# A difference moved to GpSimd, softmax sums from a 129th column, and an earlier order of the first pair's gate products

## The chip, the cores and the metric

The kernel runs on one core of one Trainium2 chip. Time is device microseconds of a whole launch, the median of three runs: 5331.07 us (5317.5 to 5331.74).

## The reference

The input is x (64 x 256 x 128: batch, nodes, features) and adj (256 x 256). Four layers follow, each x = x + layer(relu(layernorm(x))).

```python
# layer 0, five times; in_matrix = out_matrix = adj
m = adj @ h ; av = [m, m]
z = sigmoid(av @ w3.T + b3 + h @ u3.T + bu3) ; r = sigmoid(av @ w4.T + b4 + h @ u3.T + bu3)
hv = tanh(av @ w5.T + b5 + (r * h) @ u5.T + bu5)
h = (1 - z) * h + z * hv
# layer 1: relu of a projection of h, adj-hop and adj-2-hop;  layer 2: adj and a projection, divided by the row's norm
# layer 3: graph attention
e[b,i,j] = sum_e a[e] * leaky_relu(s1[b,i,e] + s2[b,j,e] + b_lin[e]) + adj[i,j]
out = sigmoid(softmax_j(e) @ h)
```

Layer 3 is the large part: for each batch element it needs 256 x 256 x 256 values of a leaky relu, each reduced with the vector a.

## The kernel before, in words

Two batch elements make a pair; there are 32 pairs. Each pair has a front (layers 0 to 2 and the preparation of layer 3, function `front`), 128 tiles of layer 3, and two tails (softmax and product for 128 of the 256 rows i, function `tail`).

**Tiles.** A tile holds, for 4 rows i, 128 of the 256 values of e (half 0 or half 1), 2 batch elements and 256 columns j: 128 partitions x 4 x 512 floats. The leaky relu is written as a linear part (`lin`, made once per pair) and a relu or a minimum. DVE (VectorE) makes a tile with one instruction (L703), ACT (ScalarE) with eight relus of 256 columns (L716), POOL (GpSimd) with eight minima of 256 columns (L723). DVE takes half 0, POOL half 1; ACT takes half 1, and half 0 only where that one is two tiles behind. PE (TensorE) reduces a tile over e with four matmuls in one of two score banks (L760). There are 4096 tiles.

**Front.** One step of layer 0 is: mix with adj (PE, L319), copy mT (ACT, L414), products with u3 and w4 into bank pr (PE), tanh for r into bank r (ACT, L422), rh = (r + 1) * hT (DVE, L426), products with w34, and with w5 and u5 into bank pv (PE, L430 to L434), tanh for z in place (ACT, L437), tanh for hv in place (ACT, L440), d = hv - hT (DVE, L445), pr = (z + 1) * d (DVE, L449), hT = 0.5 * pr + hT (DVE, L453), four transposes (PE, L459) and a copy h (ACT, L464). `norm` (L358) is the layer norm: statistics on DVE, three small operations on POOL, four relus on ACT; it is used four times a front. The banks come from a common store of three (`take`, `spare`); banks 0 and 1 hold s2a, bank 2 a copy of s2n for ACT, banks 3 and 4 the scores.

**Tail.** sc = scores + adj (DVE, L609), + lin (POOL, L613), negative row maximum (DVE, L617), two exponentials with their sums (ACT, L622), transposes (PE), a copy of the weights times 0.5 (ACT, L631), product with h3 (PE), reciprocal of the sums (DVE, L643), tanh with that as scale (ACT, L648), 0.5 * o + 0.5 and + x3 (POOL, L652 and L653), and the output DMA on SP's queue.

**The order.** While the program is written, a planner lays down the order of every engine. Each chain (a front or a tail) is a generator that yields an engine and a time from which its next step may be put; `ran(engine, us, ...)` adds a written-in price (`PROJECT` 0.86, `ELEMENTS` 0.61, `TANH` 0.57, a DVE tile 2.2, 1.05 for L613) to that engine's planned clock. The loop at the end picks the engine with the earliest clock and gives it, in this rank, a step of a tail, a step of a front, or a tile. A front may run ahead only in step with the tiles (`STEPS_OF_FRONT`, `SPREAD`, `AHEAD`); the engines hold at most 8 (DVE), 3 (ACT) and 2 (POOL) finished or begun tiles, of 13 buffers. `in_order` then fixes the order on each engine, so that at run time each goes through its list and waits where an operand isn't there. The fronts of pair 0 and pair 1 start together; no tile can be made before pair 0's is done.

Of the kernel before, what the change touches and what calls it, by code (L numbers as in the profile page):

```python
# [8 lines left out]
F32 = mybir.dt.float32  # L9
AF = mybir.ActivationFunctionType  # L10
OP = mybir.AluOpType
# [3 lines left out]
P = 128  # L15
NB = 2
# [4 lines left out]
PE, DVE, ACT, POOL = ENGINES = (mybir.EngineType.PE, mybir.EngineType.DVE, mybir.EngineType.Activation, mybir.EngineType.Pool)  # L21
# [4 lines left out]
def kernel(  # L26
# [50 lines left out]
    nc = tc.nc  # L77
    B, N, D = x.shape
    NC = N // P
    NPAIR = B // NB  # L80
# [229 lines left out]
    def project(pp, w, t, start=True, stop=True):  # L310

        side_by_side(pp, w, flat(t), start, stop)
# [8 lines left out]
    def to_feature(pt, h):  # L321

        pt = by_token(pt)
        for b in range(NB):
            for c in range(NC):
                nc.tensor.transpose(pt[:, b, c, :], h[:, b, c, :], ident)

    def to_token(pt, ht):

# [28 lines left out]
    def norm(src, since, h):  # L358

        stats = work.tile([P, NB * NC, 6], F32, name="stats")  # L360
        mv = work.tile([P, NB * NC, 2], F32, name="mv")
        s, h = rows_of(src), rows_of(h)
# [28 lines left out]
    def front(p):  # L391
# [5 lines left out]


        h = tok("h", **SHORT)
        t = yield from norm(x0, 9.0 if p else 3.0, h)  # L400
        yield PE, t, 1
        b = take()
        to_feature(b[0], h)
# [4 lines left out]
        for step in range(STEPS):  # L408
            yield PE, t_h, 1, lambda: "adj" in SET_UP
            b = take()  # L410
            mix_nodes(b[0], h, adj_t)
            t = ran(PE, MIX, t_h, b[1])
            yield ACT, t
            mT, t_m = copied("mT", b, t)  # L414
            yield PE, t_m, 1, lambda: "first" in SET_UP
            pr = take()
            project(pr[0], u3t, hT, stop=False)
            project(pr[0], w4t, mT, start=False)
            t = ran(PE, 2 * PROJECT, t_m, t_hT, pr[1])
            yield ACT, t, 1  # L420
            r = take()
# [4 lines left out]
            nc.vector.scalar_tensor_tensor(rh, by_feature(r[0]), 1.0, hT, op0=OP.add, op1=OP.mult)  # L426
            t_rh = ran(DVE, ELEMENTS, t)
            spare.append([r[0], t_rh])
            yield PE, t_rh, 1
            project(pr[0], w34, mT, start=False)  # L430
            t_z = ran(PE, PROJECT, t)
            pv = take()
            project(pv[0], w5t, mT, stop=False)
            project(pv[0], u5t, rh, start=False)  # L434
            t = ran(PE, 2 * PROJECT, t_rh, pv[1])
# [4 lines left out]
            nc.scalar.activation(pv[0], pv[0], AF.Tanh, bias=bh, scale=1.0)  # L440
            t = ran(ACT, TANH, t)

            yield DVE, t
            d = feat("d", **SHORT)
            nc.vector.tensor_sub(d, by_feature(pv[0]), hT)  # L445
            t = ran(DVE, ELEMENTS, t)
            spare.append([pv[0], t])
            yield DVE, max(t_z, clock[DVE])
            nc.vector.scalar_tensor_tensor(by_feature(pr[0]), by_feature(pr[0]), 1.0, d, op0=OP.add, op1=OP.mult)  # L449
            ran(DVE, ELEMENTS, t_z)  # L450
# [5 lines left out]
            spare.append([pr[0], t_hT])  # L456
# [86 lines left out]
        spare.append([po[0], t])  # L543


        h3 = tok("h3")
        t = yield from norm(x3, t, h3)
        yield PE, t, 1
        b = take()
# [55 lines left out]
    def tail(p, ic, pe, since, x3, h3):  # L605

        yield DVE, since
        sc = feat("sc", **SHORT)
        nc.vector.tensor_add(sc, by_feature(pe), adj_n[:, ic, :].unsqueeze(1).to_broadcast([P, NB, N]))  # L609
        t = t_pe[p * NC + ic] = ran(DVE, ELEMENTS, since)  # L610
        ops = READY[p]
        yield POOL, max(t, ops["t_lin"])
        nc.gpsimd.tensor_add(sc, sc, ops["lin"])  # L613
        t = ran(POOL, 1.05, t, ops["t_lin"])
        yield DVE, t
        nmx = work.tile([P, NB], F32, name="nmx")
        nc.vector.tensor_reduce(nmx, sc, AX.X, OP.max, negate=True)  # L617
        t = ran(DVE, ELEMENTS, t)
        yield ACT, t
        sums = work.tile([P, NB], F32, name="sums")  # L620
        for b in range(NB):
            nc.scalar.activation(sc[:, b, :], sc[:, b, :], AF.Exp, bias=nmx[:, b:b + 1], scale=1.0,  # L622
                                 accum_out=sums[:, b:b + 1])
        t_s = ran(ACT, 1.0, t)
        yield PE, t_s, 1
        b = take()
        to_token(b[0], sc)
        t = ran(PE, TURN, t_s, b[1])
        yield ACT, t
        wT = tok("wT", **SHORT)  # L630
        nc.scalar.mul(wT, by_token(b[0]), 0.5)  # L631
        t = ran(ACT, COPY, t)
        spare.append([b[0], t])
        yield PE, t, 1
        b = take()
        po = b[0][:, :NB * D].rearrange("p (b d) -> p b d", b=NB)
# [4 lines left out]
        yield DVE, t_s  # L641
        rs = work.tile([P, NB], F32, name="rs")
        nc.vector.reciprocal(rs, sums)  # L643
        t_s = ran(DVE, 0.08, t_s)
        yield ACT, max(t, t_s)
        o = work.tile([P, NB, D], F32, name="o")
        for k in range(NB):
            nc.scalar.activation(o[:, k, :], po[:, k, :], AF.Tanh, scale=rs[:, k:k + 1])  # L648
        t = ran(ACT, 0.5, t, t_s)
        spare.append([b[0], t])  # L650
        yield POOL, t
        nc.gpsimd.tensor_scalar(o, o, 0.5, 0.5, op0=OP.mult, op1=OP.add)  # L652
        nc.gpsimd.tensor_add(o, o, x3[:, :, ic, :])  # L653
        ran(POOL, 1.1, t)
# [217 lines left out]
```

## Time and profile before

| | |
|---|---|
| median of 3 runs | 5331.07 us |
| the profiled execution | 5330.89 us, span 5329.1 us |
| busy in the span | PE 5227.4, DVE 5209.6, ACT 5132.1, POOL 5153.2 us |
| tiles by engine | DVE 2009, ACT 1423, POOL 664 |
| first tile begun | POOL at 122.72, DVE at 123.51, ACT at 124.00 us |
| last score to the end | 5316.9 to 5329.1 us |

The groups are by line, engine, operation and names of the tiles; "busy" is the time in which at least one instruction of the group ran, the mean is of single instructions. Neighbouring instructions of an engine overlap in the trace, so that the distance of two starts is less than a duration. Idle time is that of the engine just before the group's instructions, with what ended it. A tile of ACT or POOL counts as eight instructions in the trace.

### The profile page before, as it was taken

The numbers are of one execution on the slowest core, as the hardware profiler recorded it, in microseconds if no ns is written. First come the engines' busy times: TensorE is split into PE (matmuls) and PEld (weight loads), VectorE is DVE, ScalarE is ACT, GpSimd is POOL, SyncE is SP. The second block draws the span as 40 slices with busy tenths as digits, with TensorE's granted clock in tenths as the row PEclk, the third lists the DMA queues.
The fourth block names the chain that finished last, engine by engine and source line by source line (L and its number), as shares of the span: only waits on it lengthen the run. The fifth ranks groups of instructions, "written<-read, shape, count | busy, mean of one in ns | idle before, by whom it ended". The sixth has DMA issues, their size and how long they took to land.

```text
span 5329.1 us, 139126 instructions
## 1 busy us (share of the span) xinstructions
PE 5227.4 (98%) x56085; PEld 1861.5 (35%) x56085; DVE 5209.6 (98%) x4313; ACT 5132.1 (96%) x13529; POOL 5153.2 (97%) x5958
## 2 busy tenths in 40 slices
PE   7999999999999999999999999999999999999998
PEld 3333333333333333333333333333333333333332
DVE  4999999999999999999999999999999999999998
ACT  4999999999999999999999999999999999999998
POOL 1999999999999999999999999999999999999999
PEclk9999999999999999999999999999999999999999
DMA  0000000000000000000000000000000000000000
GB/s 19 7 8 5 8 7 6 8 5 8 8 5 8 7 6 8 7 6 8 5 8 7 6 8 6 6 8 7 6 8 5 8 7 6 8 5 6 6 5 4
DMA packets 60344, 37.49 MB, mean 7 GB/s; under 512 B 4528, under 2 KB 59696, under 8 KB 59696
## 3 DMA queue, kind: packets, MB, share of 16 engines
q1 hardware_dynamic: 58976, 28.59, 2.3%
q8 instruction: 438, 7.18, 0.6%
q14 instruction: 210, 1.72, 0.1%
q10 hardware_dynamic: 720, 0.00, 0.0%
HBM read 18.09 MB, written 10.49 MB: 5 GB/s over the span
## 4 chain that ended last, share of the span: by engine, by line
DVE 44%; PE 31%; POOL 15%; issue 5%; ACT 5%; DMA 0%; POOLq 0%; DVEq 0%; SPq 0%; ACTq 0%
DVE rl L703 36%; PE bank L760 20%; POOL rl L723 13%; PE bank L305 10%; ACT rl L716 4%; DVE stats L365 1%; DVE bank L449 1%; DVE d L445 1%; DVE rh L426 1%; DVE hT L453 1%; PE bank L333 1%; POOL mv L300 1%; POOL sc L613 1%; DVE mv L368 1%; DVE nmx L617 0%
## 5 line engine op out<-in xcount | busy, mean ns | idle before, releaser
L723 POOL TENSOR_SCALAR rl<-s2n,s1b 128x256 f32<-128x256 f32 x5312 | 4779.4, 953 | 9.5 <-ACT s1b L590 9.3
L703 DVE TENSOR_TENSOR rl<-s1a,bank 128x2048 f32<-128x2048 f32 x2009 | 4468.7, 2275 | 11.7 <-ACT s1a L599 11.7
L716 ACT ACTIVATE rl<-bank,s1b 128x256 f32<-128x256 f32 x11072 | 4409.4, 903 | 1.0
L760 PE MATMUL bank<-rl,win_n 128*32 128x512 f32 x21384 | 2659.7, 594 | 38.0 <-DVE rl L703 31.2
L760 PE MATMUL bank<-rl,win 128*32 128x512 f32 x11384 | 1511.8, 594 | 0.0
L760 PEld LDWEIGHTS bank<-rl,win_n 128*32 128x32 f32 x21384 | 682.5, 110 | 1512.9 <-issue 1214.9
L760 PEld LDWEIGHTS bank<-rl,win 128*32 128x32 f32 x11384 | 369.1, 110 | 749.5 <-issue 618.6
L305 PE MATMUL bank<-mT,wts 128*32 128x512 f32 x2560 | 335.0, 593 | 1.4 <-DVE d L445 0.6
L305 PE MATMUL bank<-adj_t,h 128*32 128x256 f32 x5120 | 308.5, 381 | 4.6 <-ACT h L464 3.5
L305 PEld LDWEIGHTS bank<-adj_t,h 128*32 128x32 f32 x5120 | 165.2, 110 | 174.8 <-issue 52.2
L376 ACT ACTIVATE h<-x,mv 128x128 f32<-128x128 f32 x384 | 171.3, 626 | 35.5 <-POOL mv L372 35.2
L382 ACT COPY mT<-bank 128x512 f32<-128x512 f32 x160 | 146.4, 915 | 39.0 <-PE bank L305 30.5
L305 PE MATMUL bank<-hT,wts 128*32 128x512 f32 x1280 | 168.3, 593 | 0.0
L305 PE MATMUL bank<-mT,w 128*32 128x512 f32 x1280 | 166.8, 593 | 1.3 <-ACT bank L422 1.3
L305 PE MATMUL bank<-rh,u5t 128*32 128x512 f32 x1280 | 166.6, 592 | 0.0
L422 ACT ACTIVATE bank<-bank,gate_b 128x512 f32<-128x512 f32 x160 | 150.8, 942 | 13.8 <-PE bank L305 13.5
L437 ACT ACTIVATE bank<-bank,gate_b 128x512 f32<-128x512 f32 x160 | 145.9, 912 | 16.2 <-PE bank L305 16.1
L440 ACT ACTIVATE bank<-bank,gate_b 128x512 f32<-128x512 f32 x160 | 147.3, 921 | 12.0 <-PE bank L305 10.6
L464 ACT COPY h<-bank 128x512 f32<-128x512 f32 x128 | 132.2, 1033 | 19.8 <-PE bank L333 19.8
L305 PEld LDWEIGHTS bank<-mT,wts 128*32 128x32 f32 x2560 | 82.0, 110 | 196.3 <-issue 142.4
L716 ACT ACTIVATE rl<-s2c,s1a 128x256 f32<-128x256 f32 x312 | 148.5, 891 | 0.0
L300 POOL TENSOR_TENSOR mv<-mv,minus_half 128x4 f32<-128x4 f32 x128 | 133.0, 1039 | 10.7
(113 smaller groups left out, 3204.7 us busy)
## 6 DMA issues: line engine op xcount, KB each, us to landing
xin<-in_x_dram SPq DMA_DIRECT2D x64, 128.0 KB, 2.2
lin<-row SPq DMA_DIRECT2D x32, 256.0 KB, 7.6
out_dram<-o SPq DMA_DIRECT2D x64, 128.0 KB, 1.8
row<-quarter SPq DMA_DIRECT2D x32, 64.0 KB, 1.5
w_raw<-in_L_gnn_w_w_dram SPq DMA_DIRECT2D x3, 128.0 KB, 2.7
th_raw<-in_L_gnn_Theta_dram SPq DMA_DIRECT2D x1, 320.0 KB, 3.9
adj_n<-in_adj_dram SPq DMA_DIRECT2D x1, 256.0 KB, 3.5
w_raw<-in_L_gnn_u_w_dram SPq DMA_DIRECT2D x2, 64.0 KB, 2.9
```

The costliest lines, as they stand in the source:

```text
L300: nc.gpsimd.tensor_tensor(t, t, minus_half, op=OP.pow)
L305: nc.tensor.matmul(o[g:g + 32], w[:, g:g + 32], t, start=start, stop=stop, skip_group_check=True)
L376: nc.scalar.activation(h[:, k, :], s[:, k, :], AF.Relu, bias=mv[:, k, 0:1], scale=mv[:, k, 1:2])
L382: nc.scalar.copy(c, by_feature(bank[0]))
L422: nc.scalar.activation(r[0], pr[0], AF.Tanh, bias=br, scale=0.5)
L437: nc.scalar.activation(pr[0], pr[0], AF.Tanh, bias=bz, scale=0.5)
L440: nc.scalar.activation(pv[0], pv[0], AF.Tanh, bias=bh, scale=1.0)
L464: nc.scalar.copy(h, by_token(b[0]))
L703: nc.vector.tensor_tensor(t, rows.to_broadcast(whole), ops["s2a"].unsqueeze(1).to_broadcast(whole), op=OP.min)
L716: nc.scalar.activation(t[:, g, b, :], (s2p if k else ops["s2c"])[:, b, :], AF.Relu, bias=ops["s1"][k][:, b, i:i + 1], scale=-1.0)
L723: nc.gpsimd.tensor_scalar(t[:, part, b, :], ops["s2n"][:, b, :], ops["s1"][1][:, b, i:i + 1], None, op0=OP.min)
L760: nc.tensor.matmul(pe[g * 32:(g + 1) * 32, :], w[:, k, 31 - r:63 - r], flat(t[:, g]), start=first, stop=(left[block] == 0), skip_group_che ...
```

## The change

Four things change, and the planner's order with them.

1. In layer 0 of all pairs but the first, tanh for hv is written to SBUF (d), POOL subtracts hT in place, planned at 1.3 us, and the bank pv is given back after the tanh. In the first pair the difference stays on DVE.
2. h3 gets a 129th column that holds 2.0 (a memset on POOL per pair). The exponentials write no sums; the product with h3 is 129 columns wide, and its last column is twice the sum. The reciprocal reads that column from the bank, so it comes after the product. The copy of the weights isn't scaled any more.
3. In the first pair, u3's product is put as soon as hT is there, w4's and w5's as soon as mT is there, w34's after the tanh for r, u5's after rh. Its pr, r and pv are banks 3, 2 and 4, which no tile uses yet, instead of banks from the store. The front of the second and later pairs is planned to begin at 20.0 us instead of 9.0.
4. In the last tail of all, the addition of lin and the last two operations are on DVE. In the other tails the planner's price of POOL's addition of lin is 1.3 instead of 1.05 us.

```diff
-        t = yield from norm(x0, 9.0 if p else 3.0, h)
+        t = yield from norm(x0, 20.0 if p else 3.0, h)
...
+            if p == 0:
+                pr, r, pv = ([banks[k], 0.0] for k in (3, 2, 4))
+                yield PE, t_hT, 0, lambda: "first" in SET_UP
+                project(pr[0], u3t, hT, stop=False)
+                ran(PE, PROJECT, t_hT)
+                yield PE, t_m
+                project(pr[0], w4t, mT, start=False)
+                t = ran(PE, PROJECT, t_m)
+                project(pv[0], w5t, mT, stop=False)
+                ran(PE, PROJECT)
+                yield ACT, t
...
+            if p == 0:
+                yield PE, t
+                project(pr[0], w34, mT, start=False)
+                t_z = ran(PE, PROJECT, t)
+                yield PE, t_rh
+                project(pv[0], u5t, rh, start=False)
+                t = ran(PE, PROJECT, t_rh)
...
-            nc.scalar.activation(pv[0], pv[0], AF.Tanh, bias=bh, scale=1.0)
-            nc.vector.tensor_sub(d, by_feature(pv[0]), hT)
...
+            if p < 1:
+                nc.scalar.activation(pv[0], pv[0], AF.Tanh, bias=bh, scale=1.0)
+                t = ran(ACT, TANH, t)
+                yield DVE, t
+                nc.vector.tensor_sub(d, by_feature(pv[0]), hT)
+                t = ran(DVE, ELEMENTS, t)
+            else:
+                nc.scalar.activation(d, by_feature(pv[0]), AF.Tanh, bias=bh, scale=1.0)
+                t = ran(ACT, TANH, t)
+                spare.append([pv[0], t])
+                yield POOL, t
+                nc.gpsimd.tensor_sub(d, d, hT)
+                t = ran(POOL, 1.3, t)
+            yield DVE, max(t, t_z)
             nc.vector.scalar_tensor_tensor(by_feature(pr[0]), by_feature(pr[0]), 1.0, d, op0=OP.add, op1=OP.mult)
...
-        h3 = tok("h3")
+        h3 = work.tile([P, NB, NC, D + 1], F32, name="h3")
+        nc.gpsimd.memset(h3[:, :, :, D:D + 1], 2.0)
...
+        end = (p, ic) == (NPAIR - 1, NC - 1)
+        if end:
+            yield DVE, max(t, ops["t_lin"])
+            nc.vector.tensor_add(sc, sc, ops["lin"])
+            t = ran(DVE, ELEMENTS, t, ops["t_lin"])
+        else:
+            yield POOL, max(t, ops["t_lin"])
+            nc.gpsimd.tensor_add(sc, sc, ops["lin"])
+            t = ran(POOL, 1.3, t, ops["t_lin"])
...
-            nc.scalar.activation(sc[:, b, :], sc[:, b, :], AF.Exp, bias=nmx[:, b:b + 1], scale=1.0,
-                                 accum_out=sums[:, b:b + 1])
+            nc.scalar.activation(sc[:, b, :], sc[:, b, :], AF.Exp, bias=nmx[:, b:b + 1], scale=1.0)
...
-        nc.scalar.mul(wT, by_token(b[0]), 0.5)
+        nc.scalar.copy(wT, by_token(b[0]))
...
-        po = b[0][:, :NB * D].rearrange("p (b d) -> p b d", b=NB)
+        po = b[0][:, :NB * (D + 1)].rearrange("p (b d) -> p b d", b=NB)
...
-        nc.vector.reciprocal(rs, sums)
+        nc.vector.reciprocal(rs, po[:, :, D])
...
+        yield DVE if end else POOL, t
+        e = nc.vector if end else nc.gpsimd
+        e.tensor_scalar(o, o, 0.5, 0.5, op0=OP.mult, op1=OP.add)
+        e.tensor_add(o, o, x3[:, :, ic, :])
```

More of the change, by code (lines that the diff above doesn't have):

```diff
@@ L325, in to_feature @@
             for c in range(NC):
-                nc.tensor.transpose(pt[:, b, c, :], h[:, b, c, :], ident)
+                nc.tensor.transpose(pt[:, b, c, :], h[:, b, c, 0:D], ident)
     def to_token(pt, ht):
@@ L361, in norm @@
         mv = work.tile([P, NB * NC, 2], F32, name="mv")
-        s, h = rows_of(src), rows_of(h)
+        s, h = rows_of(src), rows_of(h)[:, :, 0:D]
         yield DVE, since
@@ L414, in front @@
             mT, t_m = copied("mT", b, t)
[L415 to L421, printed above, removed]
+            if p == 0:
[10 more added lines that the diff above has]
+            else:
+                yield PE, t_m, 1, lambda: "first" in SET_UP
+                pr = take()
+                project(pr[0], u3t, hT, stop=False)
+                project(pr[0], w4t, mT, start=False)
+                t = ran(PE, 2 * PROJECT, t_m, t_hT, pr[1])
+                yield ACT, t, 1
+                r = take()
             nc.scalar.activation(r[0], pr[0], AF.Tanh, bias=br, scale=0.5)
@@ L427, in front @@
             t_rh = ran(DVE, ELEMENTS, t)
[L428 to L435, printed above, removed]
+            if p == 0:
[6 more added lines that the diff above has]
+            else:
+                spare.append([r[0], t_rh])
+                yield PE, t_rh, 1
+                project(pr[0], w34, mT, start=False)
+                t_z = ran(PE, PROJECT, t)
+                pv = take()
+                project(pv[0], w5t, mT, stop=False)
+                project(pv[0], u5t, rh, start=False)
+                t = ran(PE, 2 * PROJECT, t_rh, pv[1])
             yield ACT, t_z
@@ L439, in front @@
             yield ACT, t
-            nc.scalar.activation(pv[0], pv[0], AF.Tanh, bias=bh, scale=1.0)
-            t = ran(ACT, TANH, t)
-            yield DVE, t
             d = feat("d", **SHORT)
[L445 to L448, printed above, removed]
+            if p < 1:
[4 more added lines that the diff above has]
+                t = ran(DVE, ELEMENTS, t)
+            else:
+                nc.scalar.activation(d, by_feature(pv[0]), AF.Tanh, bias=bh, scale=1.0)
[5 more added lines that the diff above has]
+            yield DVE, max(t, t_z)
             nc.vector.scalar_tensor_tensor(by_feature(pr[0]), by_feature(pr[0]), 1.0, d, op0=OP.add, op1=OP.mult)
-            ran(DVE, ELEMENTS, t_z)
+            ran(DVE, ELEMENTS, t, t_z)
             yield DVE, clock[DVE]
@@ L455, in front @@
             t_hT = ran(DVE, ELEMENTS)
-            spare.append([pr[0], t_hT])
+            if p > 0:
+                spare.append([pr[0], t_hT])
             yield PE, t_hT, 1
@@ L611, in tail @@
         ops = READY[p]
-        yield POOL, max(t, ops["t_lin"])
-        nc.gpsimd.tensor_add(sc, sc, ops["lin"])
-        t = ran(POOL, 1.05, t, ops["t_lin"])
+        end = (p, ic) == (NPAIR - 1, NC - 1)
[3 more added lines that the diff above has]
+            t = ran(DVE, ELEMENTS, t, ops["t_lin"])
+        else:
+            yield POOL, max(t, ops["t_lin"])
+            nc.gpsimd.tensor_add(sc, sc, ops["lin"])
+            t = ran(POOL, 1.3, t, ops["t_lin"])
         yield DVE, t
@@ L619, in tail @@
         yield ACT, t
-        sums = work.tile([P, NB], F32, name="sums")
         for b in range(NB):
-            nc.scalar.activation(sc[:, b, :], sc[:, b, :], AF.Exp, bias=nmx[:, b:b + 1], scale=1.0,
-                                 accum_out=sums[:, b:b + 1])
-        t_s = ran(ACT, 1.0, t)
+            nc.scalar.activation(sc[:, b, :], sc[:, b, :], AF.Exp, bias=nmx[:, b:b + 1], scale=1.0)
+        t_s = ran(ACT, 0.8, t)
         yield PE, t_s, 1
@@ L640, in tail @@
         t = ran(PE, PRODUCT, t, b[1])
-        yield DVE, t_s
+        yield DVE, t
         rs = work.tile([P, NB], F32, name="rs")
-        nc.vector.reciprocal(rs, sums)
-        t_s = ran(DVE, 0.08, t_s)
-        yield ACT, max(t, t_s)
+        nc.vector.reciprocal(rs, po[:, :, D])
+        t = t_s = ran(DVE, 0.15, t)
+        yield ACT, t
         o = work.tile([P, NB, D], F32, name="o")
         for k in range(NB):
-            nc.scalar.activation(o[:, k, :], po[:, k, :], AF.Tanh, scale=rs[:, k:k + 1])
+            nc.scalar.activation(o[:, k, :], po[:, k, 0:D], AF.Tanh, scale=rs[:, k:k + 1])
         t = ran(ACT, 0.5, t, t_s)
         spare.append([b[0], t])
[L651 to L654, printed above, removed]
+        yield DVE if end else POOL, t
+        e = nc.vector if end else nc.gpsimd
+        e.tensor_scalar(o, o, 0.5, 0.5, op0=OP.mult, op1=OP.add)
+        e.tensor_add(o, o, x3[:, :, ic, :])
+        ran(DVE, 0.6, t) if end else ran(POOL, 1.1, t)
         nc.sync.dma_start(out[p * NB:(p + 1) * NB, ic * P:(ic + 1) * P, :].rearrange("b p d -> p b d"), o)
```

## The prediction

> **What bounds the kernel now.** I read the page's busy shares first, then busy time by stretch, then the instruction groups of the long middle stretch, then one timeline of it. Time by stretch (columns: stretch, length, busy us and instructions of each engine, granted TensorE clock, DMA share, GB/s):
>
> ```profile
> 0.00:123.00 123.00, 95.49 (x1057) 39.50 (x1057) 45.09 (x125) 46.24 (x82) 9.61 (x24) 0.93 0.07 19
> 150.00:5000.00 4850.00, 4808.85 (x52044) 1712.92 (x52040) 4827.20 (x3968) 4745.67 (x12528) 4801.07 (x5545) 1.00 0.03 7
> 5317.00:5329.10 12.10, 3.12 (x36) 1.96 (x36) 1.41 (x3) 2.32 (x7) 2.39 (x3) 0.63 0.04 11
> ```
>
> There are 123 us before the first tile, in which VectorE (DVE) works 45; a middle of 4850 us in which DVE is idle 22.8 us (0.5%), TensorE (PE) 41.2, GpSimd (POOL) 48.9 and ScalarE (ACT) 104.3; and 12 us after the last score. The middle is 91% of the time, and no engine in it has 3% to spare. These groups of it (busy us, mean ns; idle us before them and who ended it) say where DVE's little idle time lies:
>
> ```profile
> L703 DVE TENSOR_TENSOR rl<-s1a,bank 128x2048 f32<-128x2048 f32 x1866 | 4152.6, 2275 | 0.0
> L449 DVE SCALAR_TENSOR_TENSOR bank<-bank,d 128x512 f32<-128x512 f32 x149 | 103.2, 693 | 2.3
> L445 DVE TENSOR_TENSOR d<-bank,hT 128x512 f32<-128x512 f32 x149 | 100.9, 677 | 0.4 <-ACT bank L440 0.4
> L617 DVE TENSOR_REDUCE nmx<-sc 128x2 f32<-128x512 f32 x59 | 40.1, 679 | 8.2 <-POOL sc L613 8.1
> L613 POOL TENSOR_TENSOR sc<-sc,lin 128x512 f32<-128x512 f32 x59 | 78.3, 1326 | 0.0
> ```
>
> DVE never waits for a tile buffer (L703: 0.0); 8.2 of its 22.8 us are waits for POOL's addition of `lin`, which the planner prices at 1.05 us. A duration overstates an operation's price, since neighbours overlap; starts give it:
>
> ```profile
> 2503.39 0.68 DVE L609 TENSOR_TENSOR sc<-bank,adj_n 128x512 f32<-128x512 f32 x1
> 2503.99 0.68 DVE L426 SCALAR_TENSOR_TENSOR rh<-bank,hT 128x512 f32<-128x512 f32 x1
> 2504.59 2.27 DVE L703 TENSOR_TENSOR rl<-s1a,bank 128x2048 f32<-128x2048 f32 x1
> ...
> 2507.05 1.30 POOL L613 TENSOR_TENSOR sc<-sc,lin 128x512 f32<-128x512 f32 x1
> 2508.30 12.62 POOL L723 TENSOR_SCALAR rl<-s2n,s1b 128x256 f32<-128x256 f32 x14
> ...
> 2508.99 6.67 DVE L703 TENSOR_TENSOR rl<-s1a,bank 128x2048 f32<-128x2048 f32 x3
> ...
> 2513.35 4.95 ACT L716 ACTIVATE rl<-bank,s1b 128x256 f32<-128x256 f32 x12
> ```
>
> So a 128x512 operation of DVE costs 0.60 (2503.99 - 2503.39), a DVE tile (6.67 - 2.275)/2 = 2.20, POOL's quarter of 256 columns (12.62 - 0.953)/13 = 0.90, POOL's 128x512 addition 1.25, up to its mean 1.33, and ACT's 256 columns (4.95 - 0.9)/11 = 0.37.
>
> **What the skill says.** SBUF — State Buffer, Who interferes with whom: a DVE instruction with at most one SBUF input doesn't contend with GpSimd. The tile (s1a from SBUF, the other operand in a bank) and `d` are such; 2.20 a tile beside an always busy POOL agrees. GPSIMD Engine Reference, Elementwise: a two-input addition takes 1.96 times as long there as on DVE; here 1326 against 679 ns, 1.95. Perfetto Trace Analysis, Identifying the Most-Contended Engine: matmul busy time is a poor measure of headroom; so I don't take PE's 98% as proof that it binds.
>
> **The change, part by part.** The counts are those of the changed program's order.
>
> *Difference on POOL.* 155 of 160 `d` leave DVE: -155 x 0.60 = -93. The planner gives the room to tiles: DVE 2009 to 2046, +37 x 2.20 = +81. POOL: +155 x 1.28 = +198 (mean of 1.25 and 1.33 less overlap), tiles 5312 to 5064 quarters: -248 x 0.90 = -223. ACT: 11384 to 11336 relus, -48 x 0.37 = -18; of them the dearer ones from SBUF fall from 312 to 16 (891 against 903 ns in the groups' means, so taken at nothing). The tanh now writes SBUF instead of a bank; the nearest row, s1a from a bank to SBUF, runs at the same pace, so 0 (+/- 0.02 x 155 = 3, on ACT, which has 104 spare). The bank pv comes free one DVE operation earlier.
>
> *129th column.* 128 accumulator reads leave ACT. Two exponentials with their reads take 2509.32 to 2510.31 = 0.99 in the timeline, two bare activations 2 x 0.4 = 0.8: -64 x 0.19 = -12. PE: 1024 matmuls one column wider, +1/128 of 71 us busy = +0.6. The reciprocal now waits for the product and reads a bank; on DVE 0.08 becomes 0.08 to 0.2, I take 0.15: +64 x 0.07 = +4.5. It lies between product and last tanh; behind it on DVE stand tiles, with buffers in reserve, and the spare bank is held longer by about this. 32 memsets of 4 columns on POOL: 0.1 each (as its constants at the start), +3.
>
> *First pair.* In the start, u3's product already ran in the shadow of the copy of mT (PE 54.20, copy 54.45 to 55.04, w4 at 55.09). Only w5's 0.86 us between w34 and u5 is on the chain: 5 x 0.86 = 4.3 us to gain. But the second pair's instructions are laid between differently. I walked the new order by hand with the durations and handoffs of the old timeline (PE to ACT 1.1 after a product's start, 2.0 after a mix; ACT copy to PE 0.64; tanh to DVE 0.70; DVE to DVE 0.72). The second step: hT 21.1, transposes 22.0, h 22.7, mix 23.4; but pair 1's norm now stands on ACT ahead of mT (25.5 to 27.15), so mT 27.15 instead of 25.4; w4 27.8, r 28.95; PE lays pair 1's mix in (29.5 to 31.2), w34 31.2, u5 32.1, tanh 33.2, d 33.9, update 34.6, hT 35.3. In the fourth step mT is ready for PE at 53.8, but pair 1's w34, w5 and u5 are ahead: w4 at 57.2. The five new hT of pair 0 start at 21.1, 35.3, 48.5, 62.2, 77.6; before 21.09, 34.63, 48.48, 62.05, 77.74. Afterwards 0.9 us is won at the theta products. The matmuls ahead of the first tile are the same in kind and number in both orders. Gain 1 us; bounds +4 and -3.
>
> *Last softmax.* sc starts at 5316.87, nmx at 5318.94; with `lin` on DVE nmx starts after 2 x 0.72 (two dependent DVE operations): -0.6. Exponentials without reads -0.2; the reciprocal in the path +0.4; the last two operations 0.42 + 0.29 on DVE (128x256 and a cheaper one by their set-up rows) instead of 0.41 + 0.72: -0.5; handoffs -0.3. Together -1.2. The last DMA is issued that much earlier; no other DMA moves on SP's queue but with its producer.
>
> *Planner's price of `lin`*, 1.05 to 1.30: POOL's 1.28 fits now. Of the 8.2 us of DVE waits I let 7 go (bounds 4 and 8).
>
> *New wait.* The update L449 (now L476) waits for POOL instead of for DVE's own `d`; behind it are hT, DVE's tiles of 2.2 us, and on PE the transposes of hT. POOL takes `d` up between quarters of 0.90 us, and DVE is planned to come when it is done, so only lateness against plan costs. The nearest row is nmx behind POOL's sc: 8.2/59 = 0.14 us each with a price 0.23 short. With a right price I take 0.03: +155 x 0.03 = +5; bounds 0 and 0.14 x 155 = 21. The old gap between d and update (2.3 us) goes.
>
> **Sum on DVE**, the engine with least room: -93 + 81 + 4.5 = -7.5; waits -7 - 2.3 + 5 = -4.3; start -1; end -1.2: -14. POOL has -22 and ACT -30 of work; ACT's waits of 104 us come partly from POOL lateness (h behind mv 27 us, nmx 13.5), so I add -3 for steadier handoffs that DVE sees through banks. -17. The profiled execution took 5330.89 (span 5329.1, 1.8 outside it); the median is 5331.07, as good as equal. 5331 - 17 = **5314**. Here 0.3% is 16 us, about what a measurement of this kernel can tell: the forecast stands on that line.
>
> **Rivals.**
> B, DVE isn't the bound alone. The three engines' work falls by 7.5 + 22 + 30 = 60, and PE idles 41 us in the middle. If the balance is shared, lateness shrinks everywhere: half of PE's 41 goes besides the 1 + 1.2 and the 7: 5331 - 30 = 5301. For: PE's waits are spread over all three engines. Against: DVE took all of half 0 but 2 tiles, and can't shed them.
> C, new waits take the room: 0.10 us at each of 155 handoffs instead of 0.03, 11 us more, and 3 for banks held longer by the reciprocal: 5328. For: the nearest row's 0.14. Against: its price was short.
> D, slower: POOL falls behind its plan. Its norm costs 0.236 + 1.039 + 0.201 and two idle gaps of 0.08, 1.6 us for the planned 1.4, four times a pair, and DVE now meets POOL five more times a pair. If each costs 0.35 us (some 0.4 of a quarter), 54 instead of 5: 5363. Slower by 0.3% is 5347, 33 above the forecast, so it decides from (33 + 5)/155 = 0.25 us each. Against: DVE waited 4.9 us in all for rn and little for mv.
>
> **Chances.** Forecast 0.45 (its own range 5307 to 5321), B 0.22, C 0.23, D 0.10. Faster by over 0.3% (under 5315): half of the forecast's and B, 0.46; within: the other half and C, 0.44; slower 0.10. Low 5294: B with all but a few of the 41 (5331 - 9 - 41 = 5281 is its end); high 5334: C at 0.14 each (21 instead of 5, and 3). Outside lie D and the rest of B, under 0.2.
>
> **What would show it.** DVE idle in the middle under 20 us; nmx behind sc under 2; the update behind POOL's d under 8; the first DVE tile at 121 to 125; POOL's d at 1.25 to 1.33 us; 12 us after the last score becoming 11. Wrong if the first tile moves by over 5 us, if DVE idles over 40, or if L703's 2.275 changes.

## The result and the profile after

The changed kernel takes **5299.72 us** (median of 4 runs, 5299.0 to 5300.57), the kernel before 5331.13 (4 runs, 5317.5 to 5331.74). The ratio is 0.9943, 95% interval 0.993 to 0.9955: faster, by 31 us where the forecast had 17. The spread of the kernel before is taken up in the last section. The profiled execution has a span of 5298.6 us, 30.5 less than before.

First the changed kernel by stretch (columns as in the prediction: length, busy us and instructions of PE, its weight loads, DVE, ACT and POOL, clock, DMA share, GB/s):

```profile
0.00:123.00 123.00, 96.47 (x1057) 39.34 (x1057) 43.12 (x121) 48.88 (x88) 18.71 (x33) 0.96 0.08 20
150.00:5000.00 4850.00, 4824.62 (x52264) 1720.98 (x52266) 4837.71 (x3868) 4730.55 (x12415) 4800.93 (x5512) 1.00 0.03 7
5287.00:5298.60 11.60, 3.39 (x37) 1.99 (x36) 2.96 (x6) 2.12 (x5) 0.00 (x0) 0.62 0.04 11
```

Length less busy time is idle time. In the middle DVE's falls from 22.8 to 12.3 us and PE's from 41.2 to 25.4, POOL's stays (48.9 and 49.1), ACT's grows from 104.3 to 119.5. For the whole span, DVE's time can be closed as an account: busy 5209.6 to 5194.6, -15.0; idle -15.5, of which the middle gives -10.5, the stretch from 5000 to 5287 us (5317 before) -4.4, the last tail behind it -2.0, and the first 150 us +1.5.

The groups of the middle that answer to those shown of before (busy us, mean ns; idle us just before them and who ended it):

```profile
L737 DVE TENSOR_TENSOR rl<-s1a,bank 128x2048 f32<-128x2048 f32 x1913 | 4250.9, 2276 | 0.0
L476 DVE SCALAR_TENSOR_TENSOR bank<-bank,d 128x512 f32<-128x512 f32 x149 | 103.0, 691 | 2.5 <-POOL d L473 2.3
L652 DVE TENSOR_REDUCE nmx<-sc 128x2 f32<-128x512 f32 x59 | 39.8, 675 | 0.4 <-POOL sc L648 0.4
L568 DVE SCALAR_TENSOR_TENSOR x<-bank,rn,x 128x128 f32<-128x128 f32 x120 | 33.6, 342 | 0.9 <-POOL rn L300 0.6
L676 DVE RECIPROCAL rs<-bank 128x2 f32<-128x2 f32 x59 | 9.7, 164 | 0.1
L473 POOL TENSOR_TENSOR d<-d,hT 128x512 f32<-128x512 f32 x150 | 196.9, 1312 | 0.3 <-ACT d L469 0.3
```

nmx waits 0.4 us for POOL instead of 8.2, the sum x behind rn (the inverse norm of layer 2, made on POOL) 0.9 instead of the 4.9 it had in the kernel before:

```profile
L540 DVE SCALAR_TENSOR_TENSOR x<-bank,rn,x 128x128 f32<-128x128 f32 x120 | 33.5, 339 | 4.9 <-POOL rn L300 4.9
```

The new wait, the update (L476) behind POOL's d, costs 2.5, about what the old gap between d and update (2.3) had cost. A DVE tile is what it was (2276 against 2275 ns) although POOL has 155 more additions with two SBUF inputs: what the Trainium skill says in SBUF — State Buffer, Who interferes with whom, of DVE instructions with at most one SBUF input agrees here too. (The page excepts the 2-port performance modes, in which DVE takes the ports it shares with GpSimd; the prediction leaves that out. Whether the small operation in the last section is such a case, no run shows.)

One handoff of it, from the timeline (start, length, engine and line):

```profile
2495.07 1.04 ACT L469 ACTIVATE d<-bank,gate_b 128x512 f32<-128x512 f32 x1
2495.22 0.67 DVE L652 TENSOR_REDUCE nmx<-sc 128x2 f32<-128x512 f32 x1
2495.82 4.47 DVE L737 TENSOR_TENSOR rl<-s1a,bank 128x2048 f32<-128x2048 f32 x2
2497.45 1.30 POOL L473 TENSOR_TENSOR d<-d,hT 128x512 f32<-128x512 f32 x1
2498.72 7.21 POOL L757 TENSOR_SCALAR rl<-s2n,s1b 128x256 f32<-128x256 f32 x8
2500.21 0.68 DVE L476 SCALAR_TENSOR_TENSOR bank<-bank,d 128x512 f32<-128x512 f32 x1
2500.81 2.27 DVE L737 TENSOR_TENSOR rl<-s1a,bank 128x2048 f32<-128x2048 f32 x1
2503.01 0.15 DVE L676 RECIPROCAL rs<-bank 128x2 f32<-128x2 f32 x1
2503.09 0.66 DVE L480 SCALAR_TENSOR_TENSOR hT<-bank,hT 128x512 f32<-128x512 f32 x1
```

What the prediction calls POOL's quarter is one of the eight minima of 256 columns that make up a tile. The tanh ends at 2496.11; POOL takes d up at 2497.45, after the four minima that its order lays ahead of it (from 2493.87), and has it ready at 2498.75. DVE makes two tiles meanwhile and comes at 2500.21, 1.5 us after that: no wait. The reciprocal, which now reads a bank, costs 0.08 from start to start (2503.09 - 2503.01).

### The profile page after: what moved, and what is told of

Its sections match the earlier page's. It is cut to its first block, busy times and chain, and to the rows that moved or that the text cites. A ratio compares the mean times of both kernels' runs of the same rounds, so it can differ in the third digit from the quotient of the medians.

```text
span 5298.6 us, 138351 instructions
## 1 busy us (share of the span) xinstructions
PE 5215.3 (98%) x56085; PEld 1855.4 (35%) x56085; DVE 5194.6 (98%) x4198; ACT 5093.4 (96%) x13353; POOL 5126.0 (97%) x5894
## 5 line engine op out<-in xcount | busy, mean ns | idle before, releaser
L757 POOL TENSOR_SCALAR rl<-s2n,s1b 128x256 f32<-128x256 f32 x5064 | 4565.0, 943 | 11.4 <-ACT s1b L619 8.9
L737 DVE TENSOR_TENSOR rl<-s1a,bank 128x2048 f32<-128x2048 f32 x2046 | 4545.1, 2276 | 10.6 <-ACT s1a L628 10.6
L750 ACT ACTIVATE rl<-bank,s1b 128x256 f32<-128x256 f32 x11320 | 4538.6, 923 | 2.5 <-PE bank L794 1.3
L794 PE MATMUL bank<-rl,win 128*32 128x512 f32 x11336 | 1493.5, 593 | 0.0
L473 POOL TENSOR_TENSOR d<-d,hT 128x512 f32<-128x512 f32 x155 | 203.3, 1311 | 53.2 <-ACT d L469 53.2
L457 ACT ACTIVATE bank<-bank,gate_b 128x512 f32<-128x512 f32 x160 | 167.0, 1044 | 19.5 <-PE bank L305 19.5
L469 ACT ACTIVATE d<-bank,gate_b 128x512 f32<-128x512 f32 x155 | 166.7, 1076 | 7.3 <-PE bank L305 7.3
L434 ACT ACTIVATE bank<-bank,gate_b 128x512 f32<-128x512 f32 x160 | 152.9, 955 | 13.4 <-PE bank L305 12.8
L300 POOL TENSOR_TENSOR mv<-mv,minus_half 128x4 f32<-128x4 f32 x128 | 133.3, 1041 | 10.7
```

The costliest lines, as they stand in the source:

```text
L300: nc.gpsimd.tensor_tensor(t, t, minus_half, op=OP.pow)
L469: nc.scalar.activation(d, by_feature(pv[0]), AF.Tanh, bias=bh, scale=1.0)
L473: nc.gpsimd.tensor_sub(d, d, hT)
L737: nc.vector.tensor_tensor(t, rows.to_broadcast(whole), ops["s2a"].unsqueeze(1).to_broadcast(whole), op=OP.min)
L750: nc.scalar.activation(t[:, g, b, :], (s2p if k else ops["s2c"])[:, b, :], AF.Relu, bias=ops["s1"][k][:, b, i:i + 1], scale=-1.0)
L757: nc.gpsimd.tensor_scalar(t[:, part, b, :], ops["s2n"][:, b, :], ops["s1"][1][:, b, i:i + 1], None, op0=OP.min)
```

## The experiments

The experiments form three sets, each measured on a chip of its own with the kernel before beside it: the four undone parts; the changed kernel again with three loads; and the price alone, the other two loads and the last version. There the kernel before takes 5318.22, 5318.48 and 5318.71 us, and the changed kernel, measured in the second set alone, 5290.53 (5 runs, 5290.45 to 5291.33; ratio 0.9948, 0.9936 to 0.996). In their profiles POOL's minima are 0.896 to 0.898 us apart, in the first two profiles 0.899; a DVE tile takes 2.20 everywhere. Below, "+" and "-" are against these 5290.53 or 5318.71. Each ratio, to the kernel before of the same set, has an interval of up to 0.0013 to both sides, 7 us; the runs of one kernel lie within 4 us, one run each of the price alone and of the kernel before apart, and differences under 2 us are taken as none. The expectations of the first set still count from the 5300 of the first measurement: only their differences are to be compared.

The theory: the kernel before lost time because POOL was behind its plan and DVE waited for it; DVE's work sets the pace, and POOL is nearly as full. The main rivals: rival B of the prediction (PE shares the bound); that the gain is the first pair's, or the column's; that the price alone is worth nothing.

### One part undone in the changed kernel

**The difference on DVE in all pairs.**

```diff
-            if p < 1:
+            if p < NPAIR:
...
                 t = ran(DVE, ELEMENTS, t)
+                if p > 0:
+                    spare.append([pv[0], t])
```

> The changed kernel (5300 us) with one part undone: the difference stays on DVE in all pairs, all else as changed. Tiles go back to DVE 2010, ACT 11392/8, POOL 5296/8. If DVE with its waits is the bound, it gets back the work it lost (busy 5194.6 to about 5208), so +13 to +18: 5313 to 5318, with DVE idle in the middle staying near 12 us. If the three engines share the bound, their work rises by 15 + 20 + 18 and a third of that is 18: 5318, so the two theories agree here and only the size of this part is read. If the planner's price was the whole gain: 5303 or less.

Measured: 5305.11 us (5303.11 to 5306.11), ratio 0.9974 (0.9964 to 0.9985), +14.6. That is in the range expected, where both theories put it. In the order DVE has 2010 tiles instead of 2046, POOL 5296 minima instead of 5064. With the 0.608 us that a difference and what it adds to the update behind it cost in the first pair of profiles (below), an estimate of DVE's work is 155 x 0.608 - 36 x 2.197 = +15.1. The trace has less: DVE is busy 5200.8 instead of 5189.3 us, +11.5, and idle 3.9 us more (in the middle 11.6 against 8.9). So most of this part is work, and a quarter of it waits.

**The sums by the accumulator, as before.** The memset, the 129th column and the late reciprocal go; the exponentials write sums and the copy is scaled by 0.5.

```diff
-            nc.scalar.activation(sc[:, b, :], sc[:, b, :], AF.Exp, bias=nmx[:, b:b + 1], scale=1.0)
-        t_s = ran(ACT, 0.8, t)
+            nc.scalar.activation(sc[:, b, :], sc[:, b, :], AF.Exp, bias=nmx[:, b:b + 1], scale=1.0,
+                                 accum_out=sums[:, b:b + 1])
+        t_s = ran(ACT, 1.0, t)
...
-        nc.vector.reciprocal(rs, po[:, :, D])
-        t = t_s = ran(DVE, 0.15, t)
+        nc.vector.reciprocal(rs, sums)
+        t_s = ran(DVE, 0.08, t_s)
```

> The changed kernel with the exponentials' accumulated sums back and no 129th column. It gives ACT 12 us of work and takes nothing worth naming from DVE (the reciprocal measured 164 against 161 ns). If DVE is the bound: 5300, no change within 2 us. If the bound is shared: a third of 12, 5304. If banks held longer by the late reciprocal cost anything: below 5298.

Measured: 5295.97 us (5294.52 to 5297.84), ratio 0.9958 (0.9946 to 0.9971), +5.4, nearer to the 4 us expected of a shared bound than to none. But the middle is the same (DVE busy 4842.39 of 4850 us, 4841.14 in the changed kernel). The loss is in one place, the last tiles, of which DVE's start and the first operation of the last tail are, in this kernel:

```profile
5239.48 33.08 DVE L738 TENSOR_TENSOR rl<-s1a,bank 128x2048 f32<-128x2048 f32 x15
5281.98 0.69 DVE L637 TENSOR_TENSOR sc<-bank,adj_n 128x512 f32<-128x512 f32 x1 [9.42 <-PE bank L795]
```

and in the changed kernel measured again:

```profile
5235.16 39.63 DVE L737 TENSOR_TENSOR rl<-s1a,bank 128x2048 f32<-128x2048 f32 x18
5277.77 0.69 DVE L638 TENSOR_TENSOR sc<-bank,adj_n 128x512 f32<-128x512 f32 x1 [2.98 <-PE bank L794]
```

DVE's last tile ends at 5272.56 (5239.48 + 33.08), 2.2 us earlier than at 5274.79, and then DVE waits 9.42 us for the last scores instead of 2.98: the tiles still missing are other engines'. So 6.4 us come from how the planner happened to deal out the last tiles, more than the whole difference. What the column itself is worth isn't shown; by this subtraction it is next to nothing.

**The old first pair.** Product order, banks and 9.0 us as before.

```diff
-        t = yield from norm(x0, 20.0 if p else 3.0, h)
+        t = yield from norm(x0, 9.0 if p else 3.0, h)
...
-            if p == 0:
+            if p < 0:
```

> The changed kernel with the first pair's products in the old order, in banks from the store, and the second pair planned from 9.0 us again. The first DVE tile came 2.6 us earlier with the change; if that is all that this part does: 5302.5, with the first DVE tile at 123.5. If the gain at the start is owed to something else (the clock granted to PE): 5300.

Measured: 5289.46 us (5289.07 to 5289.67), ratio 0.9946 (0.9933 to 0.9958), -1.1, where +2.5 with the first tile at 123.5 was expected. No gain comes from the new order of the first pair. DVE's first tile is at 120.37 with the old order and at 120.50 with the new one; with the difference on DVE (above) it is at 124.91. So the first tile comes earlier through the second pair's differences leaving DVE, not through the products.

**The old price of lin**, 1.05 instead of 1.3.

```diff
-            t = ran(POOL, 1.3, t, ops["t_lin"])
+            t = ran(POOL, 1.05, t, ops["t_lin"])
```

> The changed kernel with the planner's price of POOL's addition of lin back at 1.05 us (it takes 1.31). If the price ended POOL's lateness: nmx waits for sc come back (0.4 to about 8 us on DVE), those of x for rn as well (0.9 to 5): 5310 to 5314. If the gain comes from less work alone: 5300 to 5302.

Measured: 5299.71 us (5298.25 to 5300.84), ratio 0.9965 (0.9952 to 0.9977), +9.2. The waits are back, in the middle, as expected if the price ended POOL's lateness, though not in full: nmx 5.0 us, x behind rn 2.4, the update behind d 2.9; DVE idles 17.6 us there instead of 8.9.

```profile
L652 DVE TENSOR_REDUCE nmx<-sc 128x2 f32<-128x512 f32 x59 | 40.2, 681 | 5.0 <-POOL sc L648 4.9
```

The four undone parts give 14.6 + 5.4 - 1.1 + 9.2 = 28.1; the whole change is worth 5318.5 - 5290.5 = 28.0. That they meet so closely is in part chance, since the 5.4 are the dealing of the last tiles. The end of the last tail was undone in none of them.

### The whole change again, and the price alone

> The changed kernel as it is, for its place beside the runs of the same call. Each of the first four experiments ran on a chip where the kernel before took 5318 instead of 5331, and there POOL's quarter tile started every 0.896 us instead of 0.899 while DVE's tile stood at 2.197: 5064 x 0.003 is 15 us. If POOL sets the pace, the changed kernel moves with the chip like the kernel before, and the ratio stays at 0.994: 5287 on the faster chip, 5300 on the slower one. If DVE sets it: near 5300 on both.

That is the 5290.53 above, with the ratio at 0.9948: it lies nearer to what was expected if POOL sets the pace (5287) than to DVE alone (near 5300). With DVE's tile unchanged, the kernel became 9.2 us faster. In DVE's account of the two profiles 5.3 us of this are busy time (5194.6 to 5189.3) and 4.6 idle time, and 3.9 of the 5.3 lie in one small operation that runs in step with POOL (last section). So POOL's pace, or something that changed with it, reaches the time through DVE. Its middle, against which the experiments are read:

```profile
150.00:5000.00 4850.00, 4829.90 (x52341) 1725.83 (x52344) 4841.14 (x3875) 4731.34 (x12440) 4796.74 (x5521) 1.00 0.03 7
```

**The kernel before with the new price**, nothing else:

```diff
-        t = ran(POOL, 1.05, t, ops["t_lin"])
+        t = ran(POOL, 1.3, t, ops["t_lin"])
```

> The kernel before with one number changed: the planner's price of POOL's addition of lin is 1.30 instead of 1.05 us. The order gives POOL 5296 quarters instead of 5312 and DVE the same 2009 tiles, so hardly any work moves. Theory (POOL late against its plan was a cost of the kernel before in its own right, and the price alone takes it away): nmx's wait for POOL in the middle falls from 8.2 to under 2 us, and the time by about 9 us, what taking the price out of the changed kernel cost. Rival (the price is worth something only together with the difference on POOL; before, DVE has its full work whatever it waits for): the wait goes, and the time stays within 3 us of the kernel before.

Measured: 5307.34 us (5305.83 to 5314.41), ratio 0.9979 (0.9972 to 0.9987), -11.4 against the kernel before. Its profiled execution is the one at 5314.41, with POOL's minima 0.898 us apart, so it is to be read beside the first two profiles. Its middle, by stretch and by groups:

```profile
150.00:5000.00 4850.00, 4816.51 (x52168) 1721.71 (x52164) 4837.72 (x3976) 4761.16 (x12571) 4803.63 (x5551) 1.00 0.03 7
```

```profile
L617 DVE TENSOR_REDUCE nmx<-sc 128x2 f32<-128x512 f32 x59 | 39.9, 676 | 2.5 <-POOL sc L613 2.4
L540 DVE SCALAR_TENSOR_TENSOR x<-bank,rn,x 128x128 f32<-128x128 f32 x120 | 33.5, 338 | 1.1 <-POOL rn L300 1.0
```

DVE idles 12.3 us instead of 22.8, as little as in the changed kernel's first profile. One number in the planner, which moves two tiles from POOL to ACT, takes most of the middle's waits away; the rival that it is worth nothing alone falls. nmx's wait came to 2.5, not under 2.

### An engine loaded

Each of these adds work to one engine once a pair (32 times): an operation on a scratch tile, or on PE the s2a product a second time into the same bank. The planner doesn't know of it. What it adds is its distance from start to start.

```diff
# one of:
+        nc.gpsimd.tensor_tensor(idle_p, idle_p, minus_half, op=OP.pow)
+        nc.vector.tensor_reduce(idle_v[:, 960:961], idle_v[:, 0:960], AX.X, OP.max)
+        nc.scalar.activation(idle_a, idle_a, AF.Relu, scale=1.0)
+        project(s2a, w2n[:, 0:P], hT)
```

> The changed kernel with one more power of 128x4 on POOL per pair (1.04 us, 33 us in all), on a scratch tile that nothing waits for, without a price, so that the order of all the rest stays. If POOL sets the pace: +25 to +33 against the changed kernel of this call. If DVE sets it: POOL has 49 us idle in the middle, of which 29 lie between its own dependent operations, so +0 to +13. If all share: about a third, +11.

> The same with one more maximum over 960 columns on DVE per pair (960 columns at 0.6 us per 512 are about 1.05 us, 34 in all), unpriced. If DVE sets the pace: +28 to +34. If POOL does: DVE has 12 us idle in the middle and 3 after it, so it takes the lead once these are used up: +15 to +20 at most. If all share: +11.

> The same with one more relu of 1024 columns on ACT per pair (about 1.0 us, 32 in all), unpriced. ACT has 119 us idle in the middle, so if POOL or DVE sets the pace: +0 to +6. If all share: +11. If ACT's handoffs set it: over +20.

> The changed kernel with the s2a product of each pair done twice on PE, into the same bank and with the same values: 32 x 0.86 = 27.5 us of PE's time. Theory (DVE sets the pace, PE has room that the tiles in reserve cover): under 0.3 of it, +8 us at most, with PE idle in the middle falling from 25 us to near nothing. Rival B of the prediction (PE shares the bound, and its idle time is what shrinks): 0.7 of it or more, +19 to +28 us, and tiles' buffers held longer, seen as DVE and POOL waiting for PE.

> The kernel before with one more power of 128x4 on POOL in each pair, on a scratch tile, not priced: 32 x 0.996 = 31.9 us of POOL's time, and no other engine's. In the changed kernel the same addition cost 24.5 us, 0.77 of itself. Theory (POOL shared the pace of the kernel before at least as much as it does that of the changed one): +25 to +32 us, and DVE's waits behind POOL (nmx, x behind rn) more than double. Rival (DVE alone set the pace before; POOL's relief was worth nothing): under +12 us.

Measured:

| loaded | added us | time us (range) | ratio (interval) | more by | share |
|---|---|---|---|---|---|
| changed, DVE | 33.9 | 5323.32 (5322.72 to 5325.19) | 1.001 (1.0001 to 1.0018) | 32.8 | 0.97 |
| changed, POOL | 31.9 | 5315.01 (5314.41 to 5317.19) | 0.9994 (0.9986 to 1.0002) | 24.5 | 0.77 |
| changed, PE | 28.1 | 5296.35 (5295.36 to 5297.98) | 0.9959 (0.9946 to 0.9971) | 5.8 | 0.21 |
| changed, ACT | 30.7 | 5295.38 (5295.19 to 5295.99) | 0.9957 (0.9945 to 0.997) | 4.9 | 0.16 |
| before, POOL | 31.9 | 5346.97 (5346.78 to 5348.06) | 1.0054 (1.0041 to 1.0068) | 28.3 | 0.89 |

DVE sets the pace, POOL nearly so, PE and ACT don't. DVE alone, for which 0 to 13 us were expected of the load on POOL, doesn't fit the 24.5. Rival B's reason falls with the 0.21: PE's idle time in the middle shrinks with the load (20.1 to 5.6 us), and the time hardly grows:

```profile
150.00:5000.00 4850.00, 4844.41 (x52544) 1733.14 (x52540) 4836.29 (x3871) 4730.36 (x12426) 4793.05 (x5517) 1.00 0.03 7
```

That POOL's work comes through DVE's waits is seen in the changed kernel with POOL loaded:

```profile
L478 DVE SCALAR_TENSOR_TENSOR bank<-bank,d 128x512 f32<-128x512 f32 x149 | 103.2, 692 | 4.9 <-POOL d L475 4.1
L655 DVE TENSOR_REDUCE nmx<-sc 128x2 f32<-128x512 f32 x59 | 39.9, 677 | 8.1 <-POOL sc L651 7.9
```

and in the kernel before with POOL loaded:

```profile
L620 DVE TENSOR_REDUCE nmx<-sc 128x2 f32<-128x512 f32 x59 | 40.2, 681 | 20.2 <-POOL sc L616 20.0
L543 DVE SCALAR_TENSOR_TENSOR x<-bank,rn,x 128x128 f32<-128x128 f32 x120 | 33.5, 339 | 3.2 <-POOL rn L302 3.0
```

nmx's wait goes from 0.3 to 8.1 and from 8.2 to 20.2. The expectation that x's wait behind rn doubles too, in the kernel before, failed: 3.2, it had 4.9. (The profile of the kernel before alone has the slower minima of POOL, the loaded one the faster, so these two pairs are not wholly alike.) The two waits carry only part of the added time. In DVE's account of the changed kernel with and without the load, idle time grows by 18.6 us and busy time by 8.0; 3.8 of the latter are again the small operation of the last section.

### A version that beats both

The changed kernel with four more prices near the trace:

```diff
-        t = ran(DVE, 1.12, since)
+        t = ran(DVE, 1.35, since)
-        t = ran(POOL, 1.4, t)
+        t = ran(POOL, 1.6, t)
-        t = ran(POOL, 1.25, t)
+        t = ran(POOL, 1.35, t)
-        ran(DVE, 0.6, t) if end else ran(POOL, 1.1, t)
+        ran(DVE, 0.6, t) if end else ran(POOL, 1.2, t)
```

> The changed kernel with four more prices near what the trace shows: POOL's part of the norm 1.6 instead of 1.4, its inverse root of the row norm 1.35 instead of 1.25, its last two operations of a tail 1.2 instead of 1.1, DVE's part of the norm 1.35 instead of 1.12. The order then gives DVE 2038 tiles instead of 2046, POOL 5048 quarters instead of 5064 and ACT 80 more relus. Theory (DVE's work is the pace, and ACT has over 100 us of room): 8 tiles x 2.2 = 17.6 us leave DVE, so 10 to 17 us faster than the changed kernel, with the rest of its waits behind POOL. Rival (the changed kernel's waits are small already, and ACT or PE are too near to take up more): within 3 us of the changed kernel, DVE idle growing by what it was given.

Measured: **5279.15 us** (5277.56 to 5279.84), ratio 0.9926 (0.9913 to 0.9938), -11.4 against the changed kernel, as expected (10 to 17). By stretch:

```profile
0.00:123.00 123.00, 96.23 (x1029) 40.28 (x1033) 40.84 (x120) 44.13 (x77) 15.76 (x29) 0.91 0.07 18
150.00:5000.00 4850.00, 4842.18 (x52560) 1747.04 (x52556) 4841.53 (x3887) 4774.47 (x12567) 4795.21 (x5522) 1.00 0.03 7
```

Eight tiles less on DVE are 17.6 us of work. DVE's busy time falls by 20.9 us (5189.3 to 5168.4 of the whole span), its idle time grows by 10.1: 7.4 of them in the first 150 us, where its first tile comes at 127.69 instead of 120.50, and 2.9 ahead of the last scores (5.83 for 2.98). In the middle DVE is as little idle as before (8.5 us for 8.9): the tiles went to ACT, and no wait took the place of DVE's work. The four prices were changed together; what each is worth, and why the first tile comes later, no run shows.

## Why the prediction was right in direction and short in size

The sum of the prediction beside what the first pair of profiles shows, as DVE's account (us; "last tail" is the time after the start of the last sc, its operations included):

| step | forecast | measured |
|---|---|---|
| differences off DVE, the update behind them | -93 | -94.2 |
| 37 tiles | +81 | +81.3 |
| reciprocal | +4.5 | +0.3 |
| other work of DVE | 0 | -3.8 |
| nmx's wait | -7 | -7.8 |
| new wait for d, less the old gap | +5 - 2.3 | +0.2 |
| other waits of the middle ("steadier handoffs") | -3 | -2.9 |
| first 150 us | -1 | +1.5 |
| idle from 5000 us to the last sc | 0 | -4.0 |
| last tail | -1.2 | -1.0 |
| sum | -17 | -30.4 |

The mechanism held: DVE's work and its waits behind POOL fell. The 13.4 us that are missing are terms of the sum that were mis-sized or put at nothing: the reciprocal 4.2, DVE's idle time before the last sc 4.0, other work of DVE 3.8, the new wait 2.5, smaller terms 1.4, less 2.5 in the first 150 us.

- **Difference on POOL**: counts and prices held. In the middle of the kernel before, d and the update stood 0.634 and 0.643 us ahead of the next start (idle time left out), after the change the update stands 0.669: 0.608 x 155 = 94.2. POOL's d takes 1312 ns, 1.267 from start to start (forecast 1.25 to 1.33). DVE's own d in the first pair, which reads a bank, takes 690, so POOL needs 1.90 times as long, near the 1.96 of the Trainium skill (GPSIMD Engine Reference, Elementwise). Undone as a whole the step costs 14.6 us, of which DVE's busy time accounts for 11.5.
- **The new wait was mis-sized**: 2.5 us in the group, not 5; per handoff 2.5/149 = 0.017 us, far under rival C's 0.10 and the 0.25 at which D decides. The row it was taken from, nmx, had waited for the short price.
- **The reciprocal was mis-sized**: 0.15 was chosen between 0.08 and 0.2; it is 0.081 from start to start, 0.076 before. Reading a bank instead of SBUF costs 0.005 us here.
- **Price of lin**: right in size, and the experiments say more than the forecast did: alone it is worth 11.4 us, undone 9.2, since x behind rn loses its waits with nmx (4.9 to 1.1 by the price alone).
- **First pair: mis-sized, and for another reason.** The walked starts of the new hT (21.1, 35.3, 48.5, 62.2, 77.6) came at 21.28, 36.53, 49.67, 63.57 and 78.94, within 1.4 us, the last one later than before (77.74). The first tile is at 120.94 instead of 123.51, so 2.6 us are won and not 1. DVE has done the same operations by then but for five differences of the second pair, 4.0 us less busy time in all (45.1 to 41.1), and idles 1.5 us more: the first row of the table counts these differences in full, though DVE mostly waits in this stretch, and the +1.5 takes part of that back. Undoing the new products changes nothing (-1.1).
- **End**: from the start of sc (5287.37) to the end (5298.6) 11.2 us instead of 12.2. Right.
- **Not in the forecast**: DVE's wait for the last scores, 5.89 before and 3.38 after, makes 2.5 of the 4.0 us ahead of the last sc: the dealing of the last tiles. Of the 3.8 us of other work, 2.8 lie in the third operation of the norm (mv, L368), whose distance to the next start falls in the middle from 0.226 to 0.202 us, 118 times. It is one that runs in step with POOL (last section); why it fell just then, no run settles.
- **Chances**: half of the forecast's 0.45 and B are 0.445, the other half and C 0.455; the prediction has 0.46 and 0.44.

**The bound** was read rightly as DVE's, 0.97 of a load on it is seen, but not wholly: POOL's work counts 0.77 to 0.89. The prediction lists POOL's 48.9 us of idle time in the middle beside DVE's 22.8 and calls DVE the engine with least room; but most of POOL's isn't room. In the changed kernel these POOL groups hold 39 of them:

```profile
L300 POOL TENSOR_TENSOR mv<-mv,minus_half 128x4 f32<-128x4 f32 x118 | 122.8, 1040 | 9.8
L687 POOL TENSOR_TENSOR o<-o,x 128x256 f32<-128x256 f32 x59 | 43.4, 736 | 4.9
L299 POOL TENSOR_SCALAR mv<-mv 128x4 f32<-128x4 f32 x118 | 27.7, 235 | 10.2 <-DVE mv L367 3.0
L686 POOL TENSOR_SCALAR o<-o 128x256 f32<-128x256 f32 x59 | 24.0, 407 | 5.0
L372 POOL TENSOR_TENSOR mv<-mv 128x4 f32<-128x4 f32 x118 | 23.7, 201 | 9.3
```

Where no releaser stands behind the idle time, no other engine is seen to have ended it. L300, L372 and L687 need the operation just before them on POOL, and the gap ahead of each is 0.083 us (9.8/118; 0.079 for L372): 24.0 us in all. L299 and L686 have much the same gap behind an unrelated minimum; its cause stays open. Only 3.0 of the 39 us ended with DVE. What is left of POOL's idle time, some 13 us, is about DVE's 12.3: POOL was about as full as DVE.

**The rivals.** B's 5301 is nearest to the time, with half of its reason wrong: DVE isn't the bound alone, but its partner is POOL and not PE (0.21). C and D fall with the new wait's 0.017. Of the signs named beforehand, DVE's idle time in the middle (12.3), nmx (0.4), the update behind d (2.5), POOL's d and the last 11 us came as said; the first tile (120.94) lies just outside 121 to 125.

## What to carry to other kernels

Before counting an engine's idle time as room, look at what ended it: gaps that no other engine ended, such as those between an engine's own dependent operations, took up little of an added load here. Where a planner lays out the order, a price that is too low on one full engine costs more than the one wait in which it shows, so compare every price with the distance of starts before moving work. Before a part is credited with what undoing it costs, look at the stretch before the end: how the last tiles were dealt alone moved 6 us. And an earlier first tile isn't in itself a gain: the fastest version here begins 7 us later.

## What the runs showed of the hardware that was not expected

- POOL and ACT are not equally fast in every execution of a program. In the changed kernel's two profiles POOL's minima are 0.8986 and 0.8961 us apart, 5064 times, so some 13 us of POOL's time. ACT's neighbouring relus from a bank are 0.3576 and 0.3569 apart, which is 0.2% too; DVE's tile (2.197) is the same. The times are 5299.72 and 5290.53. The kernel before stood at 5331 us in three of its first four runs and at 5318 later, once at 5328. The runs don't test that this pace causes the difference. It isn't the chip alone. The price alone took 5314.41 us in one execution and 5306 to 5308 in the other 14, all on one chip, and there 44 minima in a row took longer (first line) than on the same chip in the kernel before with POOL loaded (second line):

```profile
1050.58 39.50 POOL L723 TENSOR_SCALAR rl<-s2n,s1b 128x256 f32<-128x256 f32 x44
1051.02 39.42 POOL L726 TENSOR_SCALAR rl<-s2n,s1b 128x256 f32<-128x256 f32 x44
```

- One small operation of DVE runs in step with POOL. It is the change of sign in the norm (mv, 128x4, in place in SBUF). Its shortest take 169 ns and stand 0.077 us ahead of the next start, its longest over 1.4 us. Of the 91 that take over 0.2 us in the kernel before, 47 end 22 to 30 ns after the end of one of POOL's instructions and 35 end 468 to 482 ns after one. If each stood at 0.077 us, the 128 would cost DVE 18 us less before and 17 less after: an estimate from the mean distances, 0.221 and 0.206. That POOL holds it up is read from these times alone; no run moved this operation. The lines are of the middle before, after, and in the changed kernel measured again:

```profile
L368 DVE TENSOR_SCALAR mv<-mv 128x4 f32<-128x4 f32 x118 | 43.2, 366 | 4.0
L368 DVE TENSOR_SCALAR mv<-mv 128x4 f32<-128x4 f32 x118 | 40.7, 345 | 4.0
L368 DVE TENSOR_SCALAR mv<-mv 128x4 f32<-128x4 f32 x118 | 37.4, 317 | 4.0
```

- A reciprocal of 128x2 costs DVE 0.081 us from a bank and 0.076 from SBUF, between other operations.
- Matmul busy time says little: PE was busy for 99.6% of the middle of the changed kernel on these chips (4829.90 of 4850 us), and took 28.1 us more for 5.8. The Trainium skill says so (Perfetto Trace Analysis, Identifying the Most-Contended Engine). It also takes occupancy as a fair measure of how near the other three are to their limit. Their order agrees (DVE 99.8%, POOL 98.9%, ACT 97.6%), but the distance says little of what a load costs: on POOL and ACT, 1.3% apart, it was seen to 0.77 and 0.16.
